# Embedding rows beside the gathers: more tiles fetched row by row from SyncE and ScalarE

## The chip, the core and the metric

The kernel runs on one NeuronCore of a Trainium2 chip. TensorE (PE) does the matmuls, VectorE (DVE) and ScalarE (ACT) the element-wise work, GpSimd (POOL) the gathers by index, SyncE (SP) only issues DMAs. Each engine works through its own instructions in order and waits for the others by semaphores; an instruction that issues a DMA takes the time of its engine's queue. The metric is the time of one execution on the device in microseconds (us), as a median of several runs.

## What is computed

A recommendation model scores 16384 users. Each has 69 item numbers and one label item; every number picks a row of 96 floats out of a table of 100,001 rows. An attention weight for each row comes from the row, the label's row and their product through a small network; the weighted rows are summed in ten groups, and three dense layers give one score. Cut to what matters:

```python
u = emb[batch_user]                      # 16384 x 69 rows of 96
ql = emb[batch_label[:, 0]]
q = jnp.broadcast_to(ql[:, None, :], u.shape)
z = jnp.concatenate([q, u, q - u, q * u], axis=-1)
h = _dice(z @ W1 + b1, a1, EPS_DICE)
att = (h @ W2 + b2) @ W3 + b3
pre = jnp.where(eff, u * att, 0.0)       # eff: the number is a real item
pooled = jnp.einsum('gf,bfe->bge', window, pre).reshape(u.shape[0], G * E)
x = jnp.concatenate([pooled, ql], axis=-1)
h = _dice(_bn_eval(x @ Wf1 + bf1, EPS_BN), af1, EPS_DICE)
h = _dice(_bn_eval(h @ Wf2 + bf2, EPS_BN), af2, EPS_DICE)
return h @ Wf3 + bf3
```

## The kernel before

The users are cut into 32 blocks of 512. A block has 69 chunks of 512 rows: 64 main chunks (8 users x 64 numbers) and 5 tail chunks (one number of all 512 users). Two chunks make a step, so there are 1104 steps (`NPAIR`). A chunk is four tiles of 128 rows x 96 floats, so there are 8832 tiles in all, numbered t = 0 to 3 in a chunk.

A step i is spread over several places of the program, written out by hand in `plan`; each engine runs its share in the order in which the plan calls it:

- `fetch(i)`: for each of the two chunks (j = 0, 1) four tiles are fetched, normally by `gather`, an indirect DMA of 128 rows issued by GpSimd (L266), into the step's buffer `u`. TensorE transposes each tile (`ptr`, L325, two buffers in PSUM). VectorE multiplies by the label's row (`quT`, L377), ScalarE copies (`uT`, L386).
- `hidden(i)`, two steps later: four matmuls into `ph` (L399, L403), a sigmoid and a scaling on ScalarE (L405, L406), a product on VectorE (`y`, L407).
- `attend_rows`, `spread` (`row`, `patt`, `rw`), once per four steps: the attention weight of each row.
- `pool(i)`, seven steps later (`POOL_LAG`): up to 16 small matmuls that read `u` again and sum the weighted rows (`acc`). After it the step's buffer `u` is free.
- The dense layers of a block (`top1`, L502, and others) are put between the steps that follow it.

`u` has 14 buffers (`upool`), so GpSimd can be ahead of the pooling by that many steps.

Some tiles are not gathered. For the chunks in `SP_CHUNKS` and `ACT_CHUNKS` the tile t = 3 (`SLOT`) is fetched as 128 single-row DMAs of 384 bytes each, issued by SyncE or by ScalarE, into a buffer of `ring` (`Singles.fetch`, L301). Where the row lies in the table comes from a register; `Singles.load` (L286) fills the registers from `offsets` in SBUF, a group of rows at a time (32 for SyncE, `2 * ACT_ROWS` for ScalarE). TensorE waits for a counted semaphore before it transposes such a tile (`wait_for_single`). The ring has 4 buffers for SyncE and 3 for ScalarE; the first row of a tile waits until TensorE has pooled the buffer's former contents.

Before, SyncE has one tile in 11 steps (98 tiles), ScalarE as well (98 tiles). SyncE has little else to do: it also loads the item numbers of four blocks at a time (`load_ids`, L151) and stores the result. ScalarE's rows lie between its activations: `scalar_rows(i, 0)` ahead of `fetch(i)`, `scalar_rows(i, 1)` behind it, six rows each, over 11 steps, so that a tile is ready two steps before its use. So 8832 - 196 = 8636 tiles are gathered, and 128 further gathers fetch the label rows (`q`).

Of the kernel before, what the change touches and what calls it, by code (L numbers as in the profile page):

```python
# [48 lines left out]

ROW_BYTES = 4 * E  # L50
SLOT = 3
SP_CHUNKS = [2 * (11 * s + 9) + 1 for s in range(98)]
SP_RING = 4
ACT_CHUNKS = [2 * (11 * s + 15) + 1 for s in range(98)]
ACT_RING = 3
ACT_ROWS = 12
ACT_STEPS = -(-P // ACT_ROWS)
SINGLES = SP_CHUNKS + ACT_CHUNKS
NSB = (len(SINGLES) + P - 1) // P
# [3 lines left out]
def chunk_of(c):  # L63

    n, k = divmod(c, NCH)
    if n == NBLK - 1 and k >= EARLY:
        k = NMAIN + k - EARLY if k < EARLY + NTAIL else k - NTAIL
    return n, k
# [47 lines left out]
def rec_kernel(  # L116
# [14 lines left out]

    const = ctx.enter_context(tc.tile_pool(name="const", bufs=1))
    ipool = ctx.enter_context(tc.tile_pool(name="ipool", bufs=2))
    upool = ctx.enter_context(tc.tile_pool(name="upool", bufs=14))
    tpool = ctx.enter_context(tc.tile_pool(name="tpool", bufs=4))
    ypool = ctx.enter_context(tc.tile_pool(name="ypool", bufs=6))
    rpool = ctx.enter_context(tc.tile_pool(name="rpool", bufs=2))
# [137 lines left out]
    class Singles:  # L275
# [19 lines left out]
        def fetch(self, s, start, stop):  # L295

            b, k = self.buffers[s % len(self.buffers)], s % NSEM
            for r in range(start, stop):
                if r % self.group == 0:
                    self.load(s, r)  # L300
                d = self.engine.dma_start(  # L301
                    out=ring[r : r + 1, b], in_=row_bytes[:, bass.ds(self.values[r], ROW_BYTES)]
                ).then_inc(self.sems[k], 16)
                tc.no_tile_sem_insts.add(d.ins.name)
                tc.declare_no_dep(d.ins, group=f"ring{b}", reason="a buffer's readers have waited for its rows")
                fresh.setdefault(b, []).append(d.ins)
            if stop == P:
                for ins in fresh.pop(b):
                    tc.add_to_no_dep_group(f"ring{b}", ins)
                self.given[k] += 16 * P  # L310
                places[self.chunks[s]] = b, self.sems[k], self.given[k]
# [246 lines left out]
    def rows_of(b, n):  # L558
        return lambda: attend_rows(b, n)

    def spread_of(b, n):
        return lambda: spread(b, n)

    def pool_of(k):
        return lambda: pool(k)

    def hidden_of(k):
        return lambda: ys.__setitem__(k, hidden(k, *hs[k]))

    def tails_of(k):  # L570
        def work():
            uT = hs.pop(k)[0]
            for j in range(2):
                if chunk_of(2 * k + j)[1] >= NMAIN:
                    attend_tail(k, j, ys[k], uT)

        return work

    def fetch_of(k, between=()):
        def work():  # L580
            for j in range(2):
                n = chunk_of(2 * k + j)[0]
                if n not in pooled:
                    pooled[n] = bpool.tile([E, G, BLK], F32, tag="pooled", name=f"pooled{n}")
                    pres[n] = xpool.tile([E, NTAIL, BLK], F32, tag="pre", name=f"pre{n}")
            u, uT, quT = fetch(k, lambda: [w() for w in between])
            us[k], hs[k] = u, (uT, quT)

        return work
# [4 lines left out]
    def at(step, *work):  # L594
        plan.setdefault(step, []).extend(work)

    by_sync = Singles("sp", nc.sync, mybir.EngineType.SP, SP_CHUNKS, 0, range(SP_RING), 32)
    for s, m in enumerate(SP_CHUNKS):
        at(max(0, m // 2 - 6), lambda s=s: by_sync.fetch(s, 0, P))

    by_scalar = Singles(
        "act",
        nc.scalar,
        mybir.EngineType.Activation,
        ACT_CHUNKS,
        len(SP_CHUNKS),
        range(SP_RING, SP_RING + ACT_RING),
        2 * ACT_ROWS,
    )
    turn = {}  # L610
    for s, m in enumerate(ACT_CHUNKS):
        for k in range(ACT_STEPS):
            turn.setdefault(m // 2 - 2 - ACT_STEPS + k, []).append((s, k * ACT_ROWS, min(P, (k + 1) * ACT_ROWS)))

    def scalar_rows(i, half):

        for s, start, stop in turn.get(i, []):
            middle = min(stop, start + ACT_ROWS // 2)
            if half == 0:
                by_scalar.fetch(s, start, middle)  # L620
            elif middle < stop:
                by_scalar.fetch(s, middle, stop)

    c = NPAIR - CLOSE
    for i in range(c):
        if i >= 3 and (i - 3) % 4 == 3:
            at(i, rows_of(i - 6, 4))
        if i >= 3:
            at(i, tails_of(i - 3))
        if i >= 4 and (i - 4) % 4 == 3:  # L630
            at(i, spread_of(i - 7, 4))
        if i >= 2:
            at(i, hidden_of(i - 2))
        at(i, lambda i=i: scalar_rows(i, 0))
        if i < c - CLOSE:
            if i >= POOL_LAG:
                at(i, pool_of(i - POOL_LAG))
        else:

            for k in {0: (-15, -14), 1: (-13,), 3: (-12, -11), 4: (-10, -9), 7: (-8, -7)}.get(i - c + 8, ()):  # L640
                at(i, pool_of(c + k))
        at(i, fetch_of(i))
        at(i, lambda i=i: scalar_rows(i, 1))

    at(c, pool_of(c - 6), pool_of(c - 5), tails_of(c - 3), hidden_of(c - 2), fetch_of(c))
    at(c + 1, tails_of(c - 2), hidden_of(c - 1), fetch_of(c + 1))
# [113 lines left out]
```

## Time and profile before

| | |
|---|---|
| Timed: median of 3 runs | 13,479.29 us (13,456.67 to 13,480.97) |
| Profiled execution | 11,010.73 us, span 11,009.0 us |
| Mean granted TensorE clock | 0.736 |
| PE busy | 8954.4 us (81%) |
| POOL busy | 8291.3 us (75%), 8764 gathers of 946 ns |
| ACT busy | 3169.5 us (29%), without issuing DMAs |
| DVE busy | 3006.0 us (27%) |
| Row DMAs issued by SyncE, by ScalarE | 12,544 each |
| DMA engines, mean busy share | about 20%, 42 GB/s |

The profile is of one execution, and that one took less time than the timed runs of the same kernel. Durations are read from the profile and sums are made against its own time; a ratio carries them to the timed runs. Busy time leaves out the issue of DMAs on SP and ACT and the time between two instructions; how much of an engine's idle time is real slack has to be read from what ended it. In the page, "issue" is time in which the engine waited for nothing that the profile shows. SPq and ACTq are the queues of SyncE and ScalarE that issue DMAs.

### The profile page before, as it was taken

Reading aid. Unit: us, or ns where it says so; the run is one execution under the profiler, and the core shown is the slowest. Engines: PE = TensorE matmul, PEld = TensorE weight load, DVE = VectorE, ACT = ScalarE, POOL = GpSimd, SP = SyncE. Lnnn points to the kernel's source line nnn. Section 1 sums busy time; section 2 is a strip of 40 time slices with the busy share of each in tenths; the row PEclk is TensorE's granted clock in tenths of the full one; section 3 lists DMA queues with packets and bytes.
Section 4 is the critical chain, followed back from the end, with each engine's and each line's share of the span. In section 5 each row is a group of like instructions: output and inputs, shape, how many; then the busy total and the mean of one; then the engine's idle time right before and its main releaser. Section 6 shows DMA issues by size and latency. Waiting matters only on the chain.

```text
span 11009.0 us, 159604 instructions
## 1 busy us (share of the span) xinstructions
PE 8954.4 (81%) x41797; PEld 4357.6 (40%) x41797; DVE 3006.0 (27%) x5327; ACT 3169.5 (29%) x4969; POOL 8291.3 (75%) x8770
## 2 busy tenths in 40 slices
PE   7887888888887888878888878788788888888788
PEld 3333433333443333434433334334334334433335
DVE  3222222222222222222222222222222222222222
ACT  2222222222222222222222222222222222232223
POOL 7777777777777777777777777777777777777776
PEclk6767777677777777777777777777777776777777
DMA  2112111121111211112111121111212112111111
GB/s 49 41 41 43 41 41 41 41 43 41 41 41 41 43 41 41 41 41 43 41 41 41 41 43 41 41 41 41 43 41 41 41 41 43 41 41 41 41 41 35
DMA packets 333393, 457.69 MB, mean 42 GB/s; under 512 B 190594, under 2 KB 191106, under 8 KB 332354
## 3 DMA queue, kind: packets, MB, share of 16 engines
q0 software_dynamic: 280448, 431.33, 18.7%
q1 hardware_dynamic: 26946, 11.28, 0.4%
q10 hardware_dynamic: 25088, 4.87, 0.3%
q8 instruction: 336, 5.51, 0.2%
q14 instruction: 575, 4.71, 0.1%
HBM read 446.74 MB, written 0.07 MB: 41 GB/s over the span
## 4 chain that ended last, share of the span: by engine, by line
POOL 49%; issue 21%; PE 17%; DMA 12%; ACT 0%; DVE 0%; ACTq 0%; POOLq 0%
POOL u L266 48%; DMA u<-in_rows,ids 12%; PE p L502 4%; PE acc L325 3%; PE ph L399 2%; PE ph L403 2%; PE ptr L325 2%; POOL q L266 1%; PE prow L414 1%; PE pa L423 1%; PE ph L396 0%; PE ph L401 0%; PE pc L348 0%; PE patt L431 0%; PE p L513 0%
## 5 line engine op out<-in xcount | busy, mean ns | idle before, releaser
L266 POOL DMA_INDIRECT u<-in_rows,ids x8636 | 8169.4, 946 | 2635.4 <-issue 2429.3
L325 PE MATMUL ptr<-ident,u 128*96 128x128 f32 x8636 | 2015.9, 334 | 1962.7 <-DMA u<-in_rows,ids 1947.6
L386 ACT COPY uT<-ptr 96x512 f32<-96x512 f32 x2208 | 1267.4, 582 | 4384.7 <-DVE quT L377 3221.7
L325 PEld LDWEIGHTS ptr<-ident,u 128*96 128x96 f32 x8636 | 1154.4, 150 | 2736.8 <-DMA u<-in_rows,ids 2299.9
L325 PEld LDWEIGHTS acc<-rw,u 128*96 128x96 f32 x16018 | 1700.9, 189 | 1200.9 <-issue 1023.8
L407 DVE TENSOR_TENSOR y<-ph,y 128x512 f32<-128x512 f32 x1104 | 763.4, 691 | 4867.9 <-ACT y L406 4691.3
L377 DVE TENSOR_TENSOR quT<-ptr,qT 96x512 f32<-96x512 f32 x2048 | 1372.4, 677 | 1969.8 <-PE ptr L325 1967.9
L325 PE MATMUL acc<-rw,u 128*96 128x20 f32 x16018 | 1807.5, 260 | 37.5 <-DVE rw L436 31.8
L399 PE MATMUL ph<-uT,A 128*64 128x512 f32 x4096 | 1662.9, 889 | 1.0 <-ACT uT L386 1.0
L403 PE MATMUL ph<-quT,wn 96*64 96x512 f32 x4416 | 1601.4, 797 | 0.0
L405 ACT ACTIVATE y<-ph 128x512 f32<-128x512 f32 x1104 | 659.1, 597 | 2692.8 <-PE ph L403 2660.9
L406 ACT ACTIVATE y<-y,wn,na1c 128x512 f32<-128x512 f32 x1104 | 898.1, 814 | 37.2
L403 PEld LDWEIGHTS ph<-quT,wn 96*64 96x64 f32 x4416 | 441.1, 189 | 1050.7 <-issue 1049.6
L502 PE MATMUL p<-pooled,wf 96*100 96x512 f32 (+1 forms) x1400 | 679.4, 633 | 0.0
L399 PEld LDWEIGHTS ph<-uT,A 128*64 128x64 f32 x4096 | 266.0, 177 | 616.8 <-issue 612.1
L470 DVE COPY pooled<-acc 96x160 f32<-96x160 f32 x1008 | 420.6, 417 | 133.4 <-PE acc L325 133.4
L414 PE MATMUL prow<-y,v 128*32 128x512 f32 x2208 | 454.7, 900 | 1.0 <-DVE y L407 1.0
L502 PE MATMUL p<-pre,V 96*100 96x512 f32 (+1 forms) x700 | 401.3, 720 | 3.7 <-DVE x L485 3.4
L502 PEld LDWEIGHTS p<-pooled,wf 96*100 96x100 f32 x1400 | 256.1, 195 | 327.6 <-issue 327.6
L436 DVE SCALAR_TENSOR_TENSOR rw<-patt,bb,wn 128x320 f32<-128x320 f32 x554 | 277.5, 542 | 210.1 <-PE patt L431 206.6
L416 ACT COPY row<-prow 128x512 f32<-128x512 f32 (+1 forms) x277 | 161.9, 584 | 432.5 <-PE prow L414 402.1
L431 PE MATMUL patt<-ident,row 128*128 128x128 f32 x1108 | 221.6, 336 | 16.4 <-DVE pre L424 14.9
(72 smaller groups left out, 2438.5 us busy)
## 6 DMA issues: line engine op xcount, KB each, us to landing
ring<-in_rows SPq DMA_DIRECT2D x12544, 0.4 KB
ring<-in_rows ACTq DMA_DIRECT2D x12544, 0.4 KB
u<-in_rows,ids POOLq DMA_INDIRECT x8636
ids<-in_idx SPq DMA_DIRECT2D x8, 560.0 KB, 3.8
q<-in_emb,ids POOLq DMA_INDIRECT x128
wf<-in_far SPq DMA_DIRECT2D x1, 1209.0 KB, 6.4
wn<-in_near SPq DMA_DIRECT2D x1, 236.0 KB, 3.7
ids<-in_idx SPq DMA_DIRECT2D x1, 140.0 KB, 2.2
```

Of the source, the lines that this page charges most:

```text
L266: nc.gpsimd.indirect_dma_start(out=dst, out_offset=None, in_=table, in_offset=bass.IndirectOffsetOnAxis(ap=index, axis=0),)
L325: ins = op(out, ring[:, at[0]].bitcast(F32) if at else u[:, 4 * (c % 2) + t, :], other, **how)
L377: nc.vector.tensor_tensor(quT[:, j, :].rearrange("e (s f) -> e s f", f=FM), ptr.rearrange("e (s f) -> e s f", f=FM), by_field(q[:, k * NS ...
L386: nc.scalar.copy(uT[j][0:E], ptr)
L399: nc.tensor.matmul(p, As[n % 2][:, k // 4, :], uT[j], start=True, stop=False)
L403: nc.tensor.matmul(p, Wp, quT[:, j, :], start=False, stop=True)
L405: nc.scalar.activation(y, ph, AF.Sigmoid, scale=S_DICE)
L406: nc.scalar.activation(y, y, AF.Identity, bias=a1c, scale=na1c)
L407: nc.vector.tensor_mul(y, ph, y)
L414: nc.tensor.matmul(pr[32 * k : 32 * (k + 1), :], v2, ys[b + k], start=True, stop=True)
L470: nc.vector.tensor_copy(pooled[n][:, :, k * NS : (k + 2) * NS].rearrange("e g s -> e s g"), pa.rearrange("e j s g -> e (j s) g"),)
L502: nc.tensor.matmul(p1, w[:, h * DH : (h + 1) * DH], x, start=(k == 0), stop=(k == KTOP - 1))
```

## The change

SyncE fetches one tile in five and a half steps instead of eleven (199 tiles instead of 98), from chunk 13 on, and has five ring buffers instead of four. ScalarE fetches one tile in eight steps instead of eleven (136 instead of 98), now at even chunks, 16 rows a step instead of 12. ScalarE's rows of a step go in three bunches of 5, 5 and 6: ahead of `fetch`, between the two chunks of `fetch` (its argument `between`, called at j = 1), and behind it. Its registers are loaded 32 at a time (`2 * ACT_ROWS`) instead of 24. `u` has 13 buffers instead of 14.

```diff
 SLOT = 3
-SP_CHUNKS = [2 * (11 * s + 9) + 1 for s in range(98)]
-SP_RING = 4
-ACT_CHUNKS = [2 * (11 * s + 15) + 1 for s in range(98)]
+SP_CHUNKS = [2 * (int(5.5 * s) + 6) + 1 for s in range(199)]
+SP_RING = 5
+ACT_CHUNKS = [2 * (8 * s + 11) for s in range(136)]
 ACT_RING = 3
-ACT_ROWS = 12
+ACT_ROWS = 16
 ACT_STEPS = -(-P // ACT_ROWS)
...
-    upool = ctx.enter_context(tc.tile_pool(name="upool", bufs=14))
+    upool = ctx.enter_context(tc.tile_pool(name="upool", bufs=13))
...
-    def scalar_rows(i, half):
+    def scalar_rows(i, third):
 
         for s, start, stop in turn.get(i, []):
-            middle = min(stop, start + ACT_ROWS // 2)
-            if half == 0:
-                by_scalar.fetch(s, start, middle)
-            elif middle < stop:
-                by_scalar.fetch(s, middle, stop)
+            by_scalar.fetch(s, start + third * ACT_ROWS // 3, start + (third + 1) * ACT_ROWS // 3)
...
-        at(i, fetch_of(i))
-        at(i, lambda i=i: scalar_rows(i, 1))
+        at(i, fetch_of(i, [lambda i=i: scalar_rows(i, 1)]))
+        at(i, lambda i=i: scalar_rows(i, 2))
```

## The prediction

> **What bounds the kernel now.** I read four views in this order: the waits of POOL, the timeline of POOL, the lag of TensorE, and the timelines of the two queues (SP and ACT) that take on more rows. The waits of POOL come first because the page's busy share (75%) looks like slack and is none:
>
> ```profile
> POOL u L266 <- issue: 2429.3, 7961, 0.3
> POOL u L266 <- DMA u<-in_rows,ids: 138.0, 452, 0.3
> POOL u L266 <- PE ptr L325: 49.8, 163, 0.3
> POOL q L266 <- DMA ids<-in_idx: 2.0, 1, 2.0
> ```
>
> The columns are total, times, longest. Apart from the 2.0 us at the start, no gather ever sat more than 0.3 us behind the one before it, whoever is named as releaser. So that 0.3 us is the cost of issuing the next gather and not a wait for anybody. The timeline of POOL says the same: the first gather, one in the middle of a burst of SyncE's rows, one while SyncE was silent, and the last.
>
> ```profile
> 3.27 1.10 POOL L266 DMA_INDIRECT q<-in_emb,ids  x1 [1.95 <-DMA ids<-in_idx]
> 4005.51 0.95 POOL L266 DMA_INDIRECT u<-in_rows,ids  x1 [0.30 <-DMA u<-in_rows,ids]
> 4006.76 0.95 POOL L266 DMA_INDIRECT u<-in_rows,ids  x1 [0.30 <-issue]
> 4070.58 0.95 POOL L266 DMA_INDIRECT u<-in_rows,ids  x1 [0.31 <-issue]
> 4071.83 0.95 POOL L266 DMA_INDIRECT u<-in_rows,ids  x1 [0.30 <-issue]
> 10967.05 0.94 POOL L266 DMA_INDIRECT u<-in_rows,ids  x1 [0.30 <-issue]
> ```
>
> There are 8636 + 128 = 8764 gathers from 3.27 to 10967.05 us, start to start (10967.05 - 3.27) / 8763 = 1.2511 us. Both pairs in the middle stand 1.25 us apart, beside 12 row DMAs or beside none. POOL is a metronome from end to end, and 10,968 of the 11,009 us are its gathers; the last 41 us are TensorE finishing the last rows. Next, TensorE:
>
> ```profile
> PE ptr L325 <- DMA u<-in_rows,ids: 1947.6, 2358, 2.8
> ```
>
> TensorE waited 1947.6 us in total for gathered rows, 1.76 us in each of the 1104 steps, never over 2.8 us at once: it follows POOL and has slack. The chain's 17% of PE is read with care: the chain hops to TensorE where one of its marks happens to fall inside POOL's 0.3 us.
>
> [...]the 1.25 us do not move beside rows. [...]The timed runs are 13,479.29 / 11,010.73 = 1.2242 times the profiled one[...]. No run here shows which clock the timed runs had; I use it as the likeliest reading, which makes all engine costs scale alike.
>
> **The change part by part.**
>
> Gathers removed. Rows by singles go from 98 + 98 = 196 tiles to 199 + 136 = 335, of 8832 tiles, and no tile is named twice (SyncE takes odd chunks, ScalarE even ones). 139 gathers go, 8764 to 8625; the built instruction stream has 8631 rows on POOL against 8770, which confirms the count. 139 x 1.2511 = 173.9 us of POOL's path.
>
> SyncE's rows. Its queue in the first 120 us and in two stretches later:
>
> ```profile
> 6.23 53.96 SPq L301 DMA_DIRECT2D ring<-in_rows  x137
> 59.97 58.85 SPq L301 DMA_DIRECT2D ring<-in_rows  x152
> 3999.88 10.20 SPq L301 DMA_DIRECT2D ring<-in_rows  x25
> 4009.85 7.99 SPq L301 DMA_DIRECT2D ring<-in_rows  x25
> SPq L301 <- PE ptr L325: 5144.2, 86, 115.8
> ```
>
> 289 rows in (59.97 + 58.85 - 6.23) = 112.6 us is 0.390 us a row with its share of the loads of 32 offsets (25 rows without a load 7.99, with one 10.20: a load is 2.2 us, a row 0.32). A tile is 128 x 0.390 = 49.9 us. Before it had 11 steps (110 us) for it, and waited over 5 ms for ring buffers. Now it has 5.5 steps of 10,835 / 1104 = 9.81 us, 54.0 us: busy 92%, 199 x 49.9 = 9930 us in total, below the span by 900 us. The ring: a tile is pooled 7 steps after its use, its buffer is needed again 5 x 5.5 = 27.5 steps after its use, so 20.5 steps (201 us) lie between, for 50 us of fetching. SyncE runs ahead, and TensorE finds its rows there. The first tile is wanted in step 6, about 80 us in by the order of gathers, and is issued by 6.2 + 49.9 = 56 us; the later ones gain 4 us each. The load of indices that SyncE also issues now stands behind the first tile, at 56 us; its first reader is the head gather of step 20 (about 200 us). Cost 0. If the cover goes, each row beyond the time of a step's share is paid in full; that is the second rival.
>
> ScalarE's rows. Two bunches and the activations ahead of each:
>
> ```profile
> 4018.92 0.81 ACT L406 ACTIVATE y<-y,wn,na1c 128x512 f32<-128x512 f32 x1
> 4018.99 1.76 ACTq L301 DMA_DIRECT2D ring<-in_rows  x6
> 4015.54 0.58 ACT L386 COPY uT<-ptr 96x512 f32<-96x512 f32 x1 [0.22 <-DVE quT L377]
> 4015.61 1.74 ACTq L301 DMA_DIRECT2D ring<-in_rows  x6
> ```
>
> A row is 1.74 / 6 = 0.29 us, and the DMAs go out 0.07 us after the activation before them starts, so they lie beside it. Rows per step 98 x 128 / 1104 = 11.4 before, 136 x 128 / 1104 = 15.8 after: 4.6 us, and 136 x 4 loads of 2.2 us make 1.1 us a step, together 5.7 (before about 4.2, with 588 loads of 24 or 8). With 3169.5 / 1104 = 2.9 us of activations it is 8.5 us of 9.81 even if nothing overlapped. The third bunch now stands between the two copies of a step: the second copy is up to 5 x 0.29 = 1.5 us late when both tiles are ready. Queued behind it are that copy and the next sigmoid; TensorE waits for the copy only when the same one of two ptr buffers comes round, a step later, and for uT two steps later. Cost 0; bound on the other side in the third rival.
>
> Ring and buffers. 14 to 13 gather buffers: a buffer is read last 7 steps after its gather's step, so POOL may be 6 steps (59 us) ahead instead of 7. TensorE trails each gather by some us (it waited for gathers in most steps), so neither is reached. Cost 0.
>
> TensorE. Its instructions stay; where a tile is a single it waits for a semaphore of SP or ACT in place of a gather's. The step gets shorter by 173.9 / 1104 = 0.16 us, out of 1.76 us of waiting. At the end it is busier: four more singles in the last 30 steps make POOL finish there some 5 us earlier, which TensorE may not follow. Loss 0 to 5 us; I take 1, since its first transpose of the last gather started right on landing.
>
> Sum: 11,010.7 - 173.9 + 1 = 10,838 us for the profiled execution. Timed: x 1.2242 = 13,268 us, a ratio of 0.9843.
>
> **The rivals.** (1) The timed runs are bound by something that the profile does not show. They take 2469 us longer; if this sits on TensorE or in landing times and not in POOL's 1.25 us, POOL waits there and removed gathers buy little. For it: the gap itself. Against it: the uniform 1.22. Time 13,479 for nothing gained, 13,370 for half of it.
>
> (2) SyncE becomes the bound, and the kernel slower. Place: the wait for SP's rows in the transposes; price: 25,472 rows in a line. At 0.390 x 1.2242 = 0.477 us a row it needs 12,160 us. From 0.521 us on (13,268 / 25,472) it is the bound, from 0.529 (13,479 / 25,472) slower than before; at 0.55 it takes 14,010 us. For it: a queue 92% full, which the trace of before never ran with ScalarE's denser rows beside it. Against it: 0.32 us a row alone or beside ACT's bunches.
>
> (3) ScalarE's order becomes the bound: its 8.5 us in line with the wait for ph (2660.9 / 1104 = 2.4 us) are 10.9 us a step, 12,070 us, timed 14,770. For it: bunches in the middle of fetch; against it: the wait for ph is idle time in which rows already issue.
>
> That fewer gathers are not removed is excluded by the count.
>
> **How the numbers follow.** Forecast 0.80, rival 1 0.10 (half of it a partial gain), rival 2 0.05, rival 3 0.05. Forecast's own range: if the extra timed cost lies outside the gathers, the gain is 174 instead of 213 us (13,305); the loss at the end adds 6; the measurement can tell 0.2% (27 us): 13,230 to 13,335. To leave no more than 2 in 10 out, it is carried to 13,375, over rival 1's half gain. Faster by over 0.2%: 0.80 + 0.04 = 0.84, within 0.2%: 0.06, slower: 0.10.
>
> **What would show it.** Right: 8625 gathers still 1.25 us apart, longest wait of POOL 0.3 us, a span near 10,835, SP's queue almost without waits for TensorE, TensorE waiting for gathers a little less. Wrong: POOL with waits of several us for TensorE (rivals 1 or 3), or transposes of ring tiles that sit idle for SP's DMA (rival 2).

## The result, and the profile after

| | before | after |
|---|---|---|
| Timed, median | 13,469.94 us (13,456.67 to 13,480.97, 4 runs) | 16,238.60 us (16,218.27 to 16,244.38, 4 runs) |
| Ratio after / before | | 1.2053, 95% interval 1.2032 to 1.2074: slower |
| Profiled execution | 11,010.73 us | 16,244.38 us, span 16,242.6 us |
| Gathers, row DMAs of SyncE, of ScalarE | 8764, 12,544, 12,544 | 8625, 25,472, 17,408 |

The forecast was 13,268 us. Note the profiled executions: that of before is 2.5 ms shorter than its timed runs, that of after agrees with its own. The chain of work that ended last, followed back from the last instruction to whatever released each one, first before and then after:

```profile
POOL 49%; issue 21%; PE 17%; DMA 12%; ACT 0%; DVE 0%; ACTq 0%; POOLq 0%
```
```profile
SPq 63%; issue 36%; PE 1%; DMA 0%; another core or an unknown queue 0%; ACT 0%; DVE 0%
```

SyncE's queue and the time between its instructions are 99% of the chain; before, the chain had 49% POOL and no SPq. The waits of after (total, times, longest; "remote" stands where the profile does not show what ended the wait):

```profile
PE ptr L325 <- DMA ring<-in_rows: 4285.1, 193, 48.8
POOL u L266 <- PE ptr L325: 2332.0, 217, 52.8
POOL u L266 <- issue: 2128.2, 6896, 5.9
POOL u L266 <- PE acc L325: 1766.5, 130, 35.7
POOL u L266 <- remote: 1304.9, 573, 4.4
SPq L301 <- PE patt L431: 0.6, 3, 0.2
```

TensorE waits 4.3 ms for rows in the ring, GpSimd waits for TensorE up to 52.8 us at once (0.3 us was its longest before), and SyncE's rows wait for nobody: the longest entry under their line is 0.6 us in total, where they waited over 5 ms for ring buffers before. The timeline shows the price of its work, the first tile and a stretch later:

```profile
6.86 165.95 SPq L301 DMA_DIRECT2D ring<-in_rows  x128
1930.03 2009.11 SPq L301 DMA_DIRECT2D ring<-in_rows  x3200
```

The first tile takes 166 us (1.30 us a row), later rows 2009.11 / 3200 = 0.628 us. The prediction had 49.9 us and 0.390 us. Over the whole run it is 16,238.6 / 25,472 = 0.637 us a row. Where does a row lose its time? In the trace SyncE's register move ahead of each row DMA takes 29 ns in most cases and the row DMA itself 228 ns, but 2,818 of the 25,474 moves take more than 0.5 us, mostly about 0.7 us; so do 3,227 of the row DMAs. More time still is lost between instructions: 6,382 gaps of over 0.4 us on SyncE, again mostly about 0.7 us, make 4.5 ms. In the first profile of before no move was over 42 ns, and SyncE had 92 such gaps, nearly all of them its waits for ring buffers. These hold-ups stand on the other engines too: 1,224 of ScalarE's 17,410 moves take more than 0.5 us, and 889 instructions of TensorE and 120 of VectorE start more than 0.4 us late with nothing shown to wait for (none and 2 in the first profile of before). GpSimd's gathers keep their 946 ns.

### The profile page after: what moved, and what is told of

Its sections match the earlier page's. It is cut to its first block, busy times and chain, and to the rows that moved or that the text cites. A ratio compares the mean times of both kernels' runs of the same rounds, so it can differ in the third digit from the quotient of the medians.

```text
span 16242.6 us, 195547 instructions
## 1 busy us (share of the span) xinstructions
PE 8932.6 (55%) x41797; PEld 4559.6 (28%) x41797; DVE 2930.7 (18%) x5327; ACT 3175.3 (20%) x4969; POOL 8160.1 (50%) x8631
## 3 DMA queue, kind: packets, MB, share of 16 engines
q0 software_dynamic: 276000, 424.49, 10.9%
## 4 chain that ended last, share of the span: by engine, by line
SPq 63%; issue 36%; PE 1%; DMA 0%; another core or an unknown queue 0%; ACT 0%; DVE 0%
SPq L301 54%; SPq L286 9%; PE p L502 0%; DMA ring<-in_rows 0%; PE acc L325 0%; PE ptr L325 0%; PE patt L431 0%; PE ph L399 0%; PE ph L403 0%; ACT y L406 0%; DVE quT L377 0%; PE prow L414 0%; ACT uT L386 0%; ACT y L405 0%
## 5 line engine op out<-in xcount | busy, mean ns | idle before, releaser
L266 POOL DMA_INDIRECT u<-in_rows,ids x8497 | 8038.1, 946 | 7943.8 <-PE ptr L325 2332.0
L325 PE MATMUL ptr<-ident,ring 128*96 128x128 f32 x335 | 128.1, 382 | 4349.0 <-DMA ring<-in_rows 4285.1
L325 PE MATMUL acc<-rw,u 128*96 128x20 f32 x15766 | 1904.0, 266 | 1017.6 <-issue 569.8
L325 PEld LDWEIGHTS acc<-rw,u 128*96 128x96 f32 x15766 | 1786.7, 198 | 2115.8 <-issue 1394.7
L325 PE MATMUL ptr<-ident,u 128*96 128x128 f32 x8497 | 1563.0, 331 | 619.7 <-issue 328.9
L377 DVE TENSOR_TENSOR quT<-ptr,qT 96x512 f32<-96x512 f32 x2048 | 1318.6, 672 | 3127.4 <-PE ptr L325 2789.5
L399 PE MATMUL ph<-uT,A 128*64 128x512 f32 x4096 | 1602.4, 827 | 56.1 <-issue 52.4
L325 PEld LDWEIGHTS ptr<-ident,ring 128*96 128x96 f32 x335 | 51.9, 155 | 4413.5 <-issue 3949.8
L502 PE MATMUL p<-pooled,wf 96*100 96x512 f32 (+1 forms) x1400 | 742.8, 668 | 71.5 <-issue 68.2
L414 PE MATMUL prow<-y,v 128*32 128x512 f32 x2208 | 613.0, 822 | 214.9 <-issue 108.9
```

The lines of the kernel that those rows point to most:

```text
L266: nc.gpsimd.indirect_dma_start(out=dst, out_offset=None, in_=table, in_offset=bass.IndirectOffsetOnAxis(ap=index, axis=0),)
L325: ins = op(out, ring[:, at[0]].bitcast(F32) if at else u[:, 4 * (c % 2) + t, :], other, **how)
L377: nc.vector.tensor_tensor(quT[:, j, :].rearrange("e (s f) -> e s f", f=FM), ptr.rearrange("e (s f) -> e s f", f=FM), by_field(q[:, k * NS ...
L399: nc.tensor.matmul(p, As[n % 2][:, k // 4, :], uT[j], start=True, stop=False)
L502: nc.tensor.matmul(p1, w[:, h * DH : (h + 1) * DH], x, start=(k == 0), stop=(k == KTOP - 1))
```

## The experiments

There are 18 runs: four groups of four, each group beside the kernel before on a chip of its own, and two single ones at the end. The figures of e1 and of e3 to e8 are of one execution each, and so is that of the kernel before beside e5 to e8; the others are medians of 2 to 17. Theories A, B and C of the first four: the engines together issue only some 12 instructions per us (A); a row DMA costs 0.64 us by itself (B); all clocks are 1.22 times slower, as the prediction had it (C).

**e1: the kernel before, unchanged, profiled again.**

> The kernel before, unchanged, for its trace beside the other runs. Theory A (there is a ceiling of about 12 instructions per us over the engines of the core: 159,604 / 13,470 = 11.8 before, 195,547 / 16,239 = 12.0 after): about 13,470 us, and this trace, unlike the first one, shows register moves on SyncE and ScalarE that last 0.7 us instead of 0.03, and GpSimd held up behind TensorE. Theory B (a row DMA that SyncE issues densely costs 0.64 us by itself): about 13,470 us, but SyncE's moves and rows short as in the first trace, since it has room. Theory C (all engine clocks are slower by 1.22 in timed runs): gathers 1.53 us apart.

13,550.3 us, with a span that agrees with the timed runs this time. Its waits and its chain, to be held against those of the first profile:

```profile
POOL u L266 <- issue: 2239.2, 7262, 3.8
POOL u L266 <- remote: 1427.5, 603, 6.0
POOL u L266 <- PE ptr L325: 807.0, 157, 43.8
SPq L301 <- remote: 1289.3, 39, 67.3
```
```profile
PE 44%; issue 20%; another core or an unknown queue 18%; DVE 6%; ACT 5%; ACTq 4%; POOL 3%; DMA 0%; DVEq 0%; SPq 0%; POOLq 0%
```

GpSimd is no metronome here: it waits for TensorE. A gather still takes 944 ns at the median (947 in the first profile), so theory C falls: the gather is no slower in this run. B falls short too, since the hold-ups are here without dense rows: 2,367 of SyncE's 12,546 moves take more than 0.5 us, as A expected. And SyncE takes

```profile
1239.65 1696.91 SPq L301 DMA_DIRECT2D ring<-in_rows  x1664
```

for 1664 rows, 1.02 us a row with its waits for buffers. Its stops of over 1.6 us ahead of a row make 2.8 ms in this trace, where they made 5.3 ms in the first: the rows took up much of the slack on which the change relied, and the first profile did not show that.

**e2: no single rows at all.**

```diff
-SP_CHUNKS = [2 * (11 * s + 9) + 1 for s in range(98)]
+SP_CHUNKS = []
-ACT_CHUNKS = [2 * (11 * s + 15) + 1 for s in range(98)]
+ACT_CHUNKS = []
```

> The kernel before without any tile fetched row by row: 8960 gathers, about 108,300 instructions. Theory A: the ceiling is worth 108,300 / 11.9 = 9,100 us and no longer binds, so GpSimd does: 8960 x 1.2511 + 44 = 11,254 us, faster than before by 16%. Theory B: SyncE was not the bound before, so 264 more gathers at the timed rate of 1.535 us, 13,770 us. Theory C: 8960 x 1.2511 x 1.2242 + 50 = 13,770 us.

13,410.8 us, ratio to before 0.9898 (0.9880 to 0.9917). So on this chip all of the single rows, before's too, bought nothing: without them the kernel takes 1.0% less, and it is the only version here that computes the same result and lies below before on chips like this. A has fallen: for these 108,448 instructions it had 11,254 us. The timeline of TensorE shows a stretch of hold-ups:

```profile
4002.77 0.18 PE L325 MATMUL acc<-rw,u 128*96 128x20 f32 x1 [0.58 <-DMA u<-in_rows,ids]
4003.48 0.18 PE L325 MATMUL acc<-rw,u 128*96 128x20 f32 x1 [0.52 <-issue]
4004.90 0.19 PE L325 MATMUL acc<-rw,u 128*96 128x20 f32 x1 [1.25 <-issue]
```

Steps of 0.71 and 1.42 us between small matmuls of 0.18 us, put down to "issue" in the last two lines: the profile shows nothing that they wait for, and still they do not start.

**e3: the changed kernel with row addresses fixed when it is built**, so that the rows need no register move and no load of offsets; the rows fetched are others.

```diff
-out=ring[r : r + 1, b], in_=row_bytes[:, bass.ds(self.values[r], ROW_BYTES)]
+out=ring[r : r + 1, b], in_=row_bytes[:, (601 * r) * ROW_BYTES : (601 * r + 1) * ROW_BYTES]
```

> The changed kernel with its 42,880 row DMAs, but from addresses fixed at build time: the values are those of other rows, and the register moves and loads of offsets are left out (about 152,700 instructions). Theory A: 152,700 / 11.9 = 12,830 us. Theory B: the rows are still issued, 25,472 x 0.64 = 16,200 us, or some 15,000 us if the move and the load were 0.1 us of it.

13,436.9 us. All 42,880 row DMAs are there, and SyncE is no longer the bound (its chain has 46% PE and no SPq): theory B falls. It needs

```profile
145.36 1299.67 SPq L301 DMA_DIRECT2D ring<-in_rows  x2816
```

0.46 us a row, some waits for ring buffers among it. Without the moves and loads around the row, SyncE has room again.

**e4: the kernel before, with satisfied semaphore waits** behind each row of SyncE's, from its ninth tile on. The source asks for three; in the trace they are one more instruction a row, 11,514 in all, and not the 23,000 that the expectation counted.

```diff
+if self.name == "sp" and s >= 8:
+    for n in range(3):
+        nc.sync.wait_ge(self.sems[(s + 3 + n) % NSEM], 16 * P)
```

> The kernel before with waits on semaphores that have long been reached, put on SyncE ahead of each row DMA: no DMA more, about 23,000 instructions more (182,600). SyncE has the room for them. Theory A: 182,600 / 11.9 = 15,300 us. Theories B and C: 13,470 us, as before.

13,701.5 us, not A's 15,300, nor the (159,604 + 11,523) / 11.9 = 14,380 that A makes of the instructions as they are. The chain now has 34% of SPq, where that of e1 had 0%: instructions that have nothing to wait for are enough to put SyncE on it, at 1.1% more time.

**e5 and e6: one half of the change each**, with 13 gather buffers: SyncE's tiles alone, ScalarE's alone. Theories of this group: D and E (the 13.4 to 13.6 ms of e1 to e3 go with the number, or with the time, of TensorE's instructions), F (a ceiling shared by all engines), G (SyncE by itself needs 0.63 us a row).

> SyncE's part of the change alone: 199 tiles and 5 ring buffers, 13 gather buffers; ScalarE fetches as before. Theory F (one ceiling of about 12 instructions per us that all engines share): about 185,700 instructions, 15,470 us. Theory G (SyncE by itself issues a row with its move and its share of the loads in 0.63 us in timed runs, whatever the others do): 25,472 x 0.63 = 16,050 us.

> ScalarE's part of the change alone: 136 tiles in three bunches, 13 gather buffers; SyncE fetches 98 tiles as before. Theory F: about 169,300 instructions, 14,100 us. Theory G: SyncE has 98 tiles in the same steps as before and nothing ends later, 13,450 to 13,600 us.

15,919.8 and 13,656.4 us, beside 13,484.4 for the kernel before: 18% and 1.3%. SyncE's part is the loss. G (16,050, and 13,450 to 13,600) is nearer than F (15,470 and 14,100), which misses both by 3%.

**e7 and e8: e2 with half of the pooling matmuls, and e2 with the hidden layer's matmuls over 256 of 512 columns.**

```diff
-            for t in range(4):
+            for t in range(2):
```
```diff
-nc.tensor.matmul(p, As[n % 2][:, k // 4, :], uT[j], start=True, stop=False)
+nc.tensor.matmul(p[:, 0:256], As[n % 2][:, k // 4, :], uT[j][:, 0:256], start=True, stop=False)
...
```

The first cut is e7's, the second is one of the like lines of e8.

> No tile fetched row by row, and of the four pooling matmuls of a chunk only two (the tiles t = 0 and 1; the sums of the other two are copies of them): TensorE has 32,800 instructions fewer of 85,800, and 1104 x 0.74 = 800 us of matmul time fewer. Theory D (the 13,406 us without single rows are TensorE held up in issuing, in proportion to its instructions): GpSimd becomes the bound, 11,250 to 11,500 us. Theory E (they are TensorE's matmul time and the waits between engines): 13,406 - 800 = 12,600 us.

> No tile fetched row by row, and the four matmuls of hidden over 256 columns instead of 512 (the weights of the other 256 are copies): as many TensorE instructions, but 1104 x 4 x 0.3 = 1300 us of matmul time fewer. Theory D: about 13,400 us still, TensorE's stalls are in its instructions. Theory E: 12,100 us.

13,304.9 and 13,284.4 us: D and E both fall. (e7 takes away 8,192 matmuls and at most as many weight loads, about half of the 32,800 instructions that its expectation names; 13,304.9 is far from the 11,500 us that D has for it.) TensorE sets the pace (in e7 GpSimd waits for `ptr` up to 40.6 us at once), but giving it less work hardly helps. The timeline of e7, here without its weight loads and some other lines, shows what it is like inside:

```profile
4002.39 1.03 PE L403 MATMUL ph<-quT,wn 96*64 96x512 f32 x4
4004.12 0.94 POOL L266 DMA_INDIRECT u<-in_rows,ids  x1 [0.30 <-issue]
4005.37 0.95 POOL L266 DMA_INDIRECT u<-in_rows,ids  x1 [0.30 <-issue]
4010.50 1.01 DVE L436 SCALAR_TENSOR_TENSOR rw<-patt,bb,wn 128x320 f32<-128x320 f32 x2 [9.84 <-remote]
4010.59 0.60 ACT L405 ACTIVATE y<-ph 128x512 f32<-128x512 f32 x1 [9.32 <-remote]
4011.11 1.15 PE L325 MATMUL acc<-rw,u 128*96 128x20 f32 x6 [7.69 <-DVE rw L436]
```

For 7 us no engine but GpSimd starts anything, though `patt` and `ph`, which VectorE and ScalarE wait for, had been computed by 4003.4. GpSimd alone starts gathers in that time, the last at 4006.62. That pointed to the gathers.

**e9 and e10: half of the gathers**, in e2 and in the changed kernel. 4544 gathers are left, label rows included.

```diff
-        ins = op(out, ring[:, at[0]].bitcast(F32) if at else u[:, 4 * (c % 2) + t, :], other, **how)
+        ins = op(out, ring[:, at[0]].bitcast(F32) if at else u[:, 4 * (c % 2) + t // 2 * 2, :], other, **how)
...
-                else:
+                elif t % 2 == 0:
                     gather(rows, u[:, 4 * j + t, :], ids[n][:, 4 * k + t : 4 * k + t + 1])
```

> No single rows, and of each four tiles of a chunk only two are gathered by GpSimd (4,480 instead of 8,960 gathers of in_rows); the other two read the first two again, so the output is that of repeated rows. TensorE, VectorE and ScalarE keep all their instructions. Theory P (the hold-ups of the other engines come from GpSimd's gathers[...]): with half the gathers they halve, and the time is TensorE's own, 9,500 to 10,500 us. Theory Q (the hold-ups come by themselves and the chain TensorE-VectorE-ScalarE is what sets 13.3 ms in every kernel here; GpSimd only follows): 12,700 to 13,400 us, hardly changed. Theory R (GpSimd's 1.25 us per gather still sets the pace between hold-ups): it falls below 12,000 us, but the hold-ups stay at some 2 ms.

> The changed kernel with all its single rows, and only two of each four tiles gathered (4,480 gathers); the other two read the first two again or the single rows, so the output is that of repeated rows. Theory G (SyncE's own instructions, some 0.63 us per row in these runs, are the bound, whatever GpSimd does): 16,000 to 16,300 us, the same as the changed kernel. Theory P (GpSimd's gathers slow SyncE's row DMAs): SyncE's row falls to 0.40 to 0.50 us and the time to 10,200 to 13,000 us.

7,812.0 and 12,336.2 us. Theory P in both, though e9 is even below its 9,500 to 10,500. In e9, TensorE's waits put down to issue are nearly gone (1000.3 and 726.0 us for these two lines in e2):

```profile
PE ptr L325 <- issue: 143.1, 156, 22.2
PE acc L325 <- issue: 42.8, 30, 8.5
```

It is TensorE's own work that sets the end of e9 (81% of the chain). In e10, with the same moves, loads and rows of SyncE as in the changed kernel, a row is

```profile
4508.74 1491.31 SPq L301 DMA_DIRECT2D ring<-in_rows  x3136
```

0.476 us instead of 0.628, with SyncE still the bound (71% SPq). Only GpSimd's gathers were taken away. Theory G, that SyncE is slow whatever GpSimd does, falls.

The trace of the changed kernel shows the same without any edit. Two stretches of 28 us, one in which GpSimd waits and starts no gather and one in which it starts 22, first all engines and then SyncE's rows:

```profile
core 0: us, PE busy (x) PEld busy (x) DVE busy (x) ACT busy (x) POOL busy (x), PEclk, DMA share, GB/s
4178.00:4206.00 28.00, 11.21 (x58) 5.08 (x59) 5.46 (x9) 6.35 (x11) 0.00 (x0) 0.61 0.01 2
4052.00:4080.00 28.00, 14.99 (x69) 8.68 (x69) 4.80 (x9) 5.73 (x9) 19.59 (x22) 0.62 0.15 37
```
```profile
4178.79 27.31 SPq L301 DMA_DIRECT2D ring<-in_rows  x67
4052.29 27.79 SPq L301 DMA_DIRECT2D ring<-in_rows  x28
```

67 rows against 28, with VectorE and ScalarE about as busy in both. It holds for the whole trace: GpSimd starts no gather for over 3 us in 320 stretches; leaving out the first us of each, SyncE takes 0.406 us a row in them and 0.764 us elsewhere, and 59 of 9,309 moves take more than 0.5 us in them, 2,759 of 16,165 elsewhere.

**e11 and e12: the changed kernel with a SyncE tile per six and per seven steps.**

> The changed kernel with a SyncE tile per six steps instead of five and a half (182 tiles, 23,296 rows). Theory G: 23,296 x 0.637 us = 14,840 us, within 150; SyncE waits for nothing. If instead something that grows with all instructions sets the time (186,000 of 195,500), 15,480 us.

> The changed kernel with a SyncE tile per seven steps (156 tiles, 19,968 rows). Theory G: SyncE would need 19,968 x 0.637 us = 12,720 us, less than the 13,300 to 13,550 us that every kernel took in which SyncE was not the bound, so 13,400 to 13,700 us and SyncE waits for ring buffers again. A time in proportion to all instructions (175,000): 14,540 us.

15,486.8 and 14,469.6 us, both more than G had. SyncE is saturated even in e12, at 14,469.6 / 19,968 = 0.725 us a row: a row has no fixed price. A fit with two prices comes close. The changed kernel and e10 differ in gathers alone, which gives (16,238.6 - 12,336.2) / (8625 - 4544) = 0.956 us per gather; the rest is (16,238.6 - 8625 x 0.956) / 25,472 = 0.314 us per row. The other runs in which SyncE was saturated test that:

| | rows of SyncE | gathers | 0.314 x rows + 0.956 x gathers | measured |
|---|---|---|---|---|
| e11 | 23,296 | 8642 | 15,577 | 15,486.8 |
| e12 | 19,968 | 8668 | 14,557 | 14,469.6 |
| e5 (fewer rows of ScalarE) | 25,472 | 8663 | 16,280 | 15,919.8 |

e11 and e12 are met to 0.6%, e5 to 2.3%. But the two figures are a fit and no prices of single things: 0.314 us is less than the 0.390 us that an undisturbed row took with its share of the loads in the first profile, and than the 0.406 us of a row without gathers beside it. The same two were also met by theory A's instruction count (15,480 and 14,540), which e2 and e10 exclude: the 191,466 instructions of e10 at 12 per us would be 15,960 us.

**e13 to e16: what of a gather costs.** A quarter of each row's bytes (e13 in the changed kernel, e15 in e2), and half of the rows of each gather (e14, e16), with as many gathers; the u buffers are cleared once. The cost goes with the bytes (theory S), with the rows (D, another one than in e7) or with the gather as such (N).

```diff
-gather(rows, u[:, 4 * j + t, :], ids[n][:, 4 * k + t : 4 * k + t + 1])
+gather(rows.rearrange("n (q e) -> (n q) e", q=4), u[:, 4 * j + t, 0 : E // 4], ids[n][:, 4 * k + t : 4 * k + t + 1])
...
-gather(rows, u[:, 4 * j + t, :], ids[n][:, 4 * k + t : 4 * k + t + 1])
+gather(rows, u[0:64, 4 * j + t, :], ids[n][0:64, 4 * k + t : 4 * k + t + 1])
```

> The changed kernel, in which each gather fetches only 24 of the 96 numbers of its 128 rows (a quarter of the bytes, the same number of rows and of gathers; the u buffers are cleared once at the start and hold zeros elsewhere). The runs so far with SyncE saturated are met by 0.314 us per row plus 0.956 us per gather. Theory S (what a gather takes from SyncE goes with its bytes): 0.24 us per gather, SyncE's sum 10,100, so GpSimd's own pace, 10,800 to 11,300 us. Theory D (it goes with its rows[...]) and theory N (it goes with the instruction): unchanged, 16,000 to 16,400 us.

> The changed kernel, in which each gather fetches 64 rows instead of 128 (half of the bytes[...], the same number of gathers; the other half of the u buffers holds zeros). Theories D and S: 0.48 us per gather, 8,000 + 4,120 = 12,120 us (11,700 to 12,600), the same as with half as many gathers. Theory N: unchanged, 16,000 to 16,400 us.

> No single rows, each gather fetches 24 of 96 numbers of its 128 rows (8,960 gathers). Theory S: the hold-ups of TensorE fall to a quarter, so GpSimd sets the pace again, 11,200 to 11,500 us. Theories D and N: 13,300 to 13,450 us as with whole rows.

> No single rows, each gather fetches 64 rows instead of 128 (8,960 gathers, the other half of the u buffers holds zeros). Theory D or S: half of the hold-ups, 7,800 us if GpSimd's gather becomes as short in proportion, at most 11,300 us if it keeps its 1.25 us. Theory N: 13,300 to 13,450 us.

17,121.1, 17,533.8, 13,635.6 and 13,678.2 us, beside 13,585.6 for the kernel before. None fell, so neither bytes nor rows are what costs (theories S and D); what is left is the gather as such (N), or something that each gather has alike. Two views of e14 show why fewer rows save little anywhere, the group of gathers and their DMA queue (packets, MB, share):

```profile
L268 POOL DMA_INDIRECT u<-in_rows,ids x8497 | 7643.9, 900 | 9646.5 <-PE acc L327 6023.9
```
```profile
q0 software_dynamic: 276000, 215.67, 6.0%
```

A gather of 64 rows takes 900 ns where one of 128 takes 946, and it makes as many packets: 276,000 / 8625 = 32, as in e13 and in the changed kernel. Whether the cost goes with the gather or with its packets these runs can't tell. That e13 and e14 are even 5 and 8% above the changed kernel N does not explain. The traces show where it lies: a row takes 0.409 and 0.423 us in stretches without gathers, as before, but 0.874 and 0.938 us elsewhere. They also put 6,392 more semaphore instructions on GpSimd's queue, and this chip's kernel before was 0.9% longer; which of these counts is not shown.

**e17: the changed kernel with half of the pooling matmuls** (the edit of e7).

> The changed kernel with all its rows and gathers, but half of the pooling matmuls (the pooled sums use two of each four tiles; 8,192 matmuls and 8,192 weight loads of TensorE fewer, 3,056 more copies on VectorE). Theory N (SyncE's 0.314 us per row plus 0.956 us per gather, whatever TensorE does): 16,240 us, 16,000 to 16,400. Theory A (all instructions of all engines share a rate of 12 per us): some 13,000 fewer instructions, 15,100 us.

10,815.7 us; the kernel before took 10,985.2 us in the same comparison (10,984.5 to 10,985.7, three runs), where every other comparison gave it 13,458 to 13,586. Neither theory expected that. As the kernel before, unchanged, took 2.5 ms less too, the difference lies in the chip or in its state at that time; this is the only comparison on that chip. It tells nothing between N and A, but more than both. The waits of GpSimd, and SyncE's timeline:

```profile
POOL u L266 <- issue: 2360.0, 7733, 0.3
POOL u L266 <- DMA u<-in_rows,ids: 160.5, 526, 0.3
POOL u L266 <- PE ptr L325: 56.5, 185, 0.3
```
```profile
6.75 49.04 SPq L301 DMA_DIRECT2D ring<-in_rows  x128
5069.24 1336.02 SPq L301 DMA_DIRECT2D ring<-in_rows  x3200
```

The metronome is back: the longest wait of a gather is 0.3 us. Here SyncE issues the very rows of the changed kernel, beside as many gathers, with 49 us for the first tile and 0.418 us a row later, waits for ring buffers among it. No move takes over 42 ns. Beside the trace of the changed kernel, which has the same instructions on SyncE, the 5.4 ms between the two spans are found: its moves took 2.8 ms there and 0.7 here, and the time between its instructions was 6.0 ms there and 2.5 here; the row DMAs themselves took 6.0 and 5.9. So in these runs the hold-ups come with both together: GpSimd's gathers, and a chip that behaves as those of the other comparisons did.

**e18: the changed kernel once more, unchanged.**

> The changed kernel once more, unchanged, beside the kernel before on the same chip. Theory N with what the last comparison showed (there the kernel before took 10,985 us, and no instruction of SyncE was held up; on all chips of the earlier comparisons it took 13,458 to 13,586): where the kernel before takes some 11,000 us, the changed kernel takes 10,800 to 10,950 us, faster by 0.5 to 1.5%, with GpSimd's gathers 1.25 us apart; where the kernel before takes some 13,500 us, 16,200 to 16,300 us again, with SyncE at 0.63 us per row. A cost of the change that has nothing to do with hold-ups would show as more than 10,985 us on the first kind of chip.

16,294.0 us beside 13,467.6, ratio 1.2099 (1.2068 to 1.2129). It was a chip of the other kind again, that of e9 to e12. So the changed kernel itself was not timed where before takes 11 ms; e17 leaves out half of the pooling.

## Why the prediction was wrong

- **The failed step: the timed runs are 1.2242 times the profiled one because "all engine costs scale alike".** They do not. A gather is 946 ns in the changed kernel's profile too, while SyncE's row goes from 0.390 to 0.637 us; the longer time is hold-ups, instructions of SyncE, ScalarE, TensorE and VectorE that are late, mostly by about 0.7 us. The prediction had slower clocks as its likeliest reading of the ratio, and said that no run showed them; e1, whose span agrees with its timed runs while a gather takes 944 ns, does not agree with such a reading. e1 shows what took the time instead: a second profile of the kernel before has GpSimd waiting for TensorE for up to 43.8 us.
- **SyncE's row**, the term that carries the error: 0.390 x 1.2242 = 0.477 us was forecast, 0.637 measured, 12,160 us against 16,238.6. That is rival 2, with its place right (TensorE waits 4.3 ms for ring rows, SyncE's rows hardly wait for anything), its point right (slower from 0.529 us on), its price too low (0.55) and its chance of 0.05 far too low. A queue 92% full by a profile that did not match the timed runs had no cover. What makes the row long is not ScalarE's denser rows, which the prediction suspected, but the gathers: with ScalarE as before (e5) the time was still 15,919.8 us, with half of the gathers (e10) it was 12,336.2.
- **Rival 1**, something that the profile does not show, was half of the truth: it was there, and it was not in GpSimd's 1.25 us. But it was priced as a gain missed, and it also took the cover from SyncE, which made it a loss.
- **Gathers removed, 139 x 1.2511 = 173.9 us**: the count was right. In e17 the gathers run from 3.3 to 10774.7 us, (10774.7 - 3.3) / 8624 = 1.249 us start to start, and the span is 10,815.6 us where 10,838 was the sum for the profiled execution. That is 0.2% off, in a run without hold-ups like the first profile, but with TensorE relieved of half of its pooling; for the changed kernel as it stands it is not shown.
- **ScalarE's rows at cost 0**: 1.3% with the hold-ups (e6, one execution beside one), so probably not 0 there, and far from rival 3's 14,770; in e17, ACTq is 0% of the chain. **13 gather buffers at cost 0**: not tried alone.
- **Rows beside gathers**: the prediction looked at one direction, whether rows disturb gathers ("the 1.25 us do not move beside rows"), and the traces agree with it: wherever a gather has 128 rows, its median is 944 to 947 ns. It did not ask about the other direction. In the first profile and e17 rows are not held up either (no move of SyncE over 42 ns); on the other chips they are (2,818 of 25,474 moves over 0.5 us in the changed kernel), and in e10 taking away half of GpSimd's gathers took 24% off the time.

What stays open: what in a chip makes a gather hold up the other engines, and by which path. In the traces with hold-ups many releasers are missing ("remote", "another core or an unknown queue"), in the two without them none; whether that is a cause or a companion was not tested. The step of 0.7 us has no explanation here. The 0.956 us per gather are a fit to SyncE's total, close to the 946 ns of the gather but not shown to be it. On which chip the first profile was taken is not on record.

## What to carry to other kernels

Where the profiled execution and the timed runs differ by more than their spread, take a second profile before scaling the first one: a uniform factor is a guess, and the slack that one profile shows may not exist in the runs that count. A queue of many small instructions (here 25,472 rows with a register move each) that was planned to be 92% full had no room for a longer row here: by the prediction's sum 0.529 us instead of 0.477 is enough to lose the gain, and 0.637 was measured. Count the instructions around each row too: with fixed addresses (e3) the same rows went out at 0.46 us instead of 0.63. And where a queue slows down without a wait to blame, compare its stretches in which another engine is silent with the rest of the same trace, and take work away from the other engines one at a time: here fewer gathers of GpSimd sped up SyncE, and smaller ones did not.

## What was not expected of the hardware

- The same kernel took 10,985 us on one chip and 13,458 to 13,586 us in the six other comparisons, at nearly the same granted TensorE clock (0.735 to 0.739, and 0.721 to 0.732 in those of e1 to e16 and e18).
- In the eight traces of the second kind in which SyncE is the bound, a row of SyncE took 0.38 to 0.42 us in stretches of over 3 us without a gather, and 0.60 to 0.94 us elsewhere. A quarter of a gather's bytes, or half of its rows, did not lower that.
- A gather of 64 rows took 900 ns, one of 128 rows 946 ns: as an estimate from these two, 0.7 ns per row on a base of some 850 ns.
- The granted TensorE clock rose from 0.724 in e2 to 0.919 in e9 with half of the gathers, and fell to 0.652 in e8 with half of the hidden layer's columns. No run explains it.
